# The ending of a cross-attention kernel: one power on GpSimd for root and reciprocal, block products ahead, half the bias by TensorE, two store queues

## The chip, the cores and the metric

The kernel runs on one core of a Trainium2 chip. The metric is the device time of one execution in microseconds (us), the median of the runs. The core has five engines that run side by side and wait for each other through semaphores: TensorE (PE; its weight loads are shown as PEld), VectorE (DVE), ScalarE (ACT), GpSimd (POOL) and SyncE (SP). SP, ACT and POOL have queues from which DMA transfers are issued (SPq, ACTq, POOLq in the profile).

## The reference

A batch of 8 inputs `x` (112 rows, 320 channels) attends to a context of 375 rows with 512 channels, of which the last 4 are prompts. There are 20 heads of 16 channels. Cut to what matters:

```python
q = heads(x @ W_q);  k_t = heads(text @ W_k);  v_t = heads(text @ W_v)
probs_t  = softmax(q @ k_t^T * scale)                  # over the 371 text rows
text_out = probs_t @ v_t
k_ip = heads(ip @ W_k_ip);  v_ip = heads(ip @ W_v_ip)  # the 4 prompts
qsem = l2norm(probs_t @ text)                          # x / max(|x|, 1e-12)
sem  = qsem @ l2norm(ip)^T
probs_ip = softmax(q @ k_ip^T * scale + 0.5 * sem) * spatial_mask
out = (text_out + probs_ip @ v_ip) @ W_out + b_out + x
```

## The kernel before

All of it is float32. The work is cut into 40 steps, 8 batches with 5 rounds of 4 heads each. In a round TensorE makes the scores, VectorE their maxima, ScalarE the exponentials `p` with a copy of each row's maximum taken off; a DMA and VectorE's 32x32 transposes turn `p` into `xgT`, and TensorE multiplies it (L761) with `u`, which holds for the batch the products of the context's rows with each other beside the prompts' normalised rows, a column of ones and the head's values. So one product gives, for a head, what is needed for the norm of `qsem` (first 371 columns, summed against `p` by VectorE in `reduced`, L814, into `ss`) and 21 value columns: 4 prompt similarities, the sum of the exponentials `z`, and 16 values. ScalarE copies these 21 into `pvs` (`value_sums`, L788).

PE, SP, DVE, ACT and POOL carry out the instructions in the order in which the program writes them: after the prologue the schedule is written by hand. Two generators write a batch's last part in pieces: `finish(b)` for batches 0 to 6 and `ending(b, bd)` for batch 7, advanced by `run(before, ...)` and `next(last)` at the end of the program, where batch 6's remaining pieces and batch 7's are dealt out between each other.

What the ending does for batch 7, with the names that the prediction uses:

- `divided` (L951): the values over `z` into `attn`; first for 16 heads on GpSimd, then for the last 4 on VectorE.
- `turned_attention` (L966): TensorE transposes `attn` by chunks of 128 channels into `ps_a` (two full ones first, the third later), ScalarE copies them to `aT`.
- `bd` holds the prompts' values, each head's block in its own rows. TensorE transposes it (`ps_bT`, L984), ScalarE copies it (`bT`), and TensorE multiplies the blocks by `W_out` (`ps_bw`, L1004), copied to `bw`. With it the prompts' part of the output is a single product of the prompt weights and `bw`.
- The prompts' softmax: `z2` (GpSimd), `rn` = max(z2 * eps^2, ss) on VectorE (L993), its root on ScalarE (L994) with the table of functions switched back to Exp behind it (L995), its reciprocal on VectorE (L1018), then four operations on `fu`, Exp on ScalarE (`ex`, L1025), and three operations to the weights `w` (L1033). TensorE transposes `w` (L1037), ScalarE copies it (`wT`, L1039).
- `projected` (L1010): `aT` times `W_out` into two halves of 160 columns, `ps_o_0` and `ps_o_1`, over the full chunks first and the third later; then `wT` times `bw` on top (L1042).
- VectorE adds the input with the bias (`xb`, which lies in a part of the tile named `bd`) to each half (L1047), and SP stores each (L1048).

Between these stand batch 6's last pieces: GpSimd's sums into `attn` (L903), its transposes (L908), its copy (L912), its product with `W_out` (L917) and its output sum (L923).

PSUM tiles are handed out by the pools `mm`, `sc` and `qd` in turn; a new tile waits until the readers of the bank's last tile are done.

Of the kernel before, what the change touches and what calls it, by code (L numbers as in the profile page):

```python
# [8 lines left out]
F32 = mybir.dt.float32  # L9
AF = mybir.ActivationFunctionType  # L10
ALU = mybir.AluOpType
# [3 lines left out]
NIP = 4  # L15
SEM_SCALE = 0.5
EPS = 1e-12
# [3 lines left out]
def kernel(  # L21
# [14 lines left out]
    nc = tc.nc  # L36
    P = 128
# [13 lines left out]
    RG = 32  # L51
# [177 lines left out]
    for i in range(NX):  # L229
        xt = const.tile([P, QN, TP], F32, tag=f"xg_{i}", name=f"xg_{i}")  # L230
        nc.gpsimd.memset(xt, 0.0)
        x_ring.append(xt)

    attn_ring = []
    for i in range(2):
        attn_ring.append(const.tile([S, CP], F32, tag=f"attn_{i}", name=f"attn_{i}"))
# [2 lines left out]
    def more_constants():  # L239
        halves(1)  # L240
        halves(2)
        nc.gpsimd.memset(wo_sb[REST:, FULL, :], 0.0)
        for at in attn_ring:
            nc.gpsimd.memset(at[:, C:], 0.0)
# [685 lines left out]
    def ending(b, bd):  # L930


        s = st[b]
        eng = nc.gpsimd
        h0 = FULL * HC

        def sm(name):
            return small.tile([S, H], F32, tag=name, name=f"{name}_{b}", bufs=1)

        def sm4(name):  # L940
            return small.tile([S, H, NIP], F32, tag=name, name=f"{name}_{b}", bufs=1)
# [9 lines left out]
        def divided(on, part):  # L951
            n = part.stop - part.start
            nc.vector.reciprocal(zr[:, part], z[:, part])
            on.tensor_tensor(
                attn[:, :C].rearrange("p (h d) -> p h d", d=D)[:, part],
                pvs[:, part, NIP + 1 :],
                zr[:, part].unsqueeze(2).to_broadcast([S, n, D]),
                ALU.mult,
            )

        divided(eng, slice(0, h0))
        yield

        aT = work.tile([P, NC, S], F32, tag="aT", name=f"aT_{b}")

        def turned_attention(chunks):  # L966
            ps = bank(f"ps_a_{b}_{chunks.start}")
            for i in chunks:
                nc.tensor.transpose(
                    ps[:, i * S : (i + 1) * S], attn[:, i * P : (i + 1) * P], ident[:S, :S]  # L970
                )
            at = slice(chunks.start, chunks.stop)
            nc.scalar.copy(
                aT[:, at],
                ps[:, at.start * S : at.stop * S].rearrange("p (i s) -> p i s", s=S),
            )

        turned_attention(range(FULL))
        yield


        ps = bank("ps_bT", spare=True)
        for i in range(NC):
            nc.tensor.transpose(  # L984
                ps[:, i * HN : (i + 1) * HN], bd[:HN, i * P : (i + 1) * P], ident[:HN, :HN]
            )
        bT = work.tile([P, NC, 2 * S], F32, tag="xT", name="bT", bufs=1)[:, :, :HN]
        nc.scalar.copy(bT, ps[:, : NC * HN].rearrange("p (i k) -> p i k", k=HN))
        yield

        z2, rn = sm("z2"), sm("rn")
        eng.tensor_tensor(z2, z, z, ALU.mult)
        nc.vector.scalar_tensor_tensor(rn, z2, EPS * EPS, s["ss"], ALU.mult, ALU.max)  # L993
        nc.scalar.activation(rn, rn, AF.Sqrt)  # L994
        nc.scalar.preload_act_table(AF.Exp)  # L995
        divided(nc.vector, slice(h0, H))
        yield

        turned_attention(range(FULL, NC))
        ps_bw = bank("ps_bw")  # L1000
        for i in range(NC):

            own = slice(i * RG, min((i + 1) * RG, HN))
            nc.tensor.matmul(  # L1004
                ps_bw[own, :C], bT[:, i, own], wo_sb[:, i, :], start=True, stop=True
            )
        ps_o = [bank(f"ps_o_{b}_0", spare=True)]
        ps_o.append(ps_qd.tile([P, 512], F32, tag="qd", name=f"ps_o_{b}_1"))

        def projected(chunks):  # L1010
            for ps, part in zip(ps_o, parts):
                for i in chunks:
                    nc.tensor.matmul(  # L1013
                        ps[:S, part], aT[:, i, :], wo_sb[:, i, part], start=(i == 0), stop=False
                    )

        projected(range(FULL))
        nc.vector.reciprocal(rn, rn)  # L1018
        fu, ex, w = sm4("fu"), sm4("ex"), sm4("w")
        nc.vector.tensor_tensor(fu, pvs[:, :, :NIP], over_ip(rn), ALU.mult)  # L1020
# [4 lines left out]
        nc.scalar.activation(ex, fu, AF.Exp)  # L1025
        bw = work.tile([S, NIP, H, D], F32, tag="wv", name="bw", bufs=1)
        bw = bw.rearrange("p n h d -> p n (h d)")[:HN, 0, :]
        nc.scalar.copy(bw, ps_bw[:HN, :C])
        yield

        nc.vector.tensor_reduce(sx, ex, AX.X, ALU.add)
        nc.vector.reciprocal(rx, sx)
        nc.vector.scalar_tensor_tensor(w, ex, sm_sb, over_ip(rx), ALU.mult, ALU.mult)  # L1033
        yield

        ps = bank(f"ps_wT_{b}")
        nc.tensor.transpose(ps[:HN, :S], w.rearrange("s h n -> s (h n)"), ident[:S, :S])  # L1037
        wT = work.tile([P, NE, TP], F32, tag="ctxT", name=f"wT_{b}")[:, 0, :S]
        nc.scalar.copy(wT[:HN], ps[:HN, :S])  # L1039
        projected(range(FULL, NC))  # L1040
        for ps, part in zip(ps_o, parts):
            nc.tensor.matmul(ps[:S, part], wT[:HN], bw[:, part], start=False, stop=True)  # L1042
        yield

        ob = work.tile([S, C], F32, tag="xb", name=f"ob_{b}", bufs=1)
        for ps, part in zip(ps_o, parts):
            nc.vector.tensor_tensor(ob[:, part], ps[:S, part], s["xb"][:, part], ALU.add)  # L1047
            nc.sync.dma_start(out[b, :, part], ob[:, part])  # L1048
        del st[b]
        yield  # L1050

# [350 lines left out]
    for g in range(NG):  # L1402
        if g == 1:
            run(("f", b - 2), None)
        for j, _ in enumerate(multiplied(b, g)):
            coming(g, places.get(g, {}).get(j, ()))
            if g == 0 and j == 2:
                transposed(b, g + 1)
            if g == 1 and j == 2:
                run(before, None)  # L1410
                own_channels(bd)
                transposed(b, g + 1)
            if g == 1 and j == 4:
# [49 lines left out]
    run(before, None, 2)  # L1463
    drain(last)
# [44 lines left out]
```

## Time and profile before

| | us |
|---|---|
| median of 3 runs | 409.94 |
| lowest and highest run | 409.65, 410.64 |
| the profiled execution: its span, first to last instruction | 409.5 |
| busy: TensorE | 402.0 |
| busy: VectorE | 333.5 |
| busy: ScalarE | 191.4 |
| busy: GpSimd | 127.6 |

The profile names a group or an instruction by its line in the kernel, its engine, its operation and its tiles (out<-in). In a timeline the first number is the start in us from the span's beginning, the second the length; equal neighbours are merged, with the first start, the whole length and their number. A note in brackets gives the engine's idle time before it and who ended it. A float32 matrix product is two instructions on TensorE, a transpose is one. The chain of waits is followed back from the last instruction: at each step to what released it, or to the instruction before it on its engine.

Some groups of the same page that frame the ending, by line, engine and operation, with count, busy time and mean length of one:

```profile
L761 PE MATMUL ps_qd<-u,xgT 32*112 32x136 f32 (+11 forms) x3840 | 216.4, 352 | 1.5 <-POOL u L679 1.1
L814 DVE CUSTOM_DVE_ANT_0 p<-ps_qd,p 112x371 f32<-112x371 f32 x152 | 73.6, 541 | 12.1 <-ACT pvs L788 7.4
L788 ACT COPY pvs<-ps_qd 112x21 f32<-112x21 f32 x152 | 21.8, 200 | 56.7 <-DVE ss L814 50.4
```

### The profile page before, as it was taken

To read this page: it belongs to the slowest core of one execution; us is meant where nothing else is said; L and a number is where in the kernel's file an instruction comes from. 1 tells how busy PE (TensorE), PEld (TensorE's weight loads), DVE (VectorE), ACT (ScalarE), POOL (GpSimd) and SP (SyncE) were. 2 spreads that over 40 slices of the span, in tenths; PEclk is the share of its full clock that TensorE was granted. 3 is DMA by queue.
4 is the path that set the end of the run, shared out by engine and by line. 5 is a ranking of instruction groups with operands and counts; after the bars stand their busy time and mean duration, and the time that the engine had idled before them with its cause. 6 is when DMAs were issued, how large, how long until landed. Compare 5 with 4: busy or idle time off the path is not lost.

```text
span 409.5 us, 14124 instructions
## 1 busy us (share of the span) xinstructions
PE 402.0 (98%) x5603; PEld 316.1 (77%) x5603; DVE 333.5 (81%) x705; ACT 191.4 (47%) x676; POOL 127.6 (31%) x294
## 2 busy tenths in 40 slices
PE   8998999999999999999999999999999999999996
PEld 8866687978777877878686877778777878787894
DVE  4354589877999898896899898887799988878985
ACT  3253234344533743434643574333734485346763
POOL 7203311322281153011154136002037135104681
PEclk9999999999999999999999999999999999999999
DMA  8876957799666866677646776666756444666310
GB/s 234 166 188 170 231 145 193 170 196 208 150 162 163 215 141 177 156 165 163 180 115 167 177 174 161 166 160 161 180 152 173 114 123 121 191 159 179 106 49 28
DMA packets 59332, 65.83 MB, mean 161 GB/s; under 512 B 20165, under 2 KB 52793, under 8 KB 59268
## 3 DMA queue, kind: packets, MB, share of 16 engines
q1 hardware_dynamic: 55326, 59.11, 58.4%
q0 software_dynamic: 1456, 3.14, 3.5%
q10 hardware_dynamic: 2486, 2.69, 2.1%
q8 instruction: 44, 0.72, 0.8%
q14 instruction: 20, 0.16, 0.1%
HBM read 20.22 MB, written 5.22 MB: 62 GB/s over the span
## 4 chain that ended last, share of the span: by engine, by line
PE 92%; DMA 3%; SPq 2%; POOL 1%; ACT 1%; issue 0%; DVE 0%; POOLq 0%
PE ps_qd L761 44%; PE ps_v L598 12%; PE ps_k L559 10%; PE ps_g L529 7%; PE ps_s L713 6%; PE ps_q L391 3%; PE ps_o L917 3%; DMA wip<-in_L_xattn_W_v_ip_dram 3%; PE ps_k L576 2%; PE ps_g L491 1%; SPq L737 1%; PE ps_w L477 1%; PE ps_c L460 1%; SPq L543 1%; PE ps_q L373 1%; PE ps_o L1013 0%
## 5 line engine op out<-in xcount | busy, mean ns | idle before, releaser
L761 PE MATMUL ps_qd<-u,xgT 32*112 32x136 f32 (+11 forms) x3840 | 216.4, 352 | 1.5 <-POOL u L679 1.1
L761 PEld LDWEIGHTS ps_qd<-u,xgT 32*112 32x112 f32 x3840 | 178.1, 172 | 36.4 <-issue 7.1
L749 DVE STREAM_TRANSPOSE xgT<-xg 128x768 f32<-128x768 f32 (+1 forms) x63 | 123.1, 1972 | 5.4 <-DMA xg<-p 5.1
L730 ACT ACTIVATE p<-ps_s,nmx 112x371 f32<-112x371 f32 x160 | 85.7, 585 | 56.9 <-DVE nmx L726 55.7
L726 DVE TENSOR_REDUCE nmx<-ps_s 112x1 f32<-112x371 f32 x160 | 77.2, 534 | 30.8 <-PE ps_s L713 28.9
L679 POOL COPY u<-vr 128x64 f32<-128x64 f32 x120 | 26.8, 237 | 190.9 <-PE ps_qd L761 113.8
L814 DVE CUSTOM_DVE_ANT_0 p<-ps_qd,p 112x371 f32<-112x371 f32 x152 | 73.6, 541 | 12.1 <-ACT pvs L788 7.4
L713 PE MATMUL ps_s<-kT,qm 32*112 32x375 f32 (+1 forms) x320 | 62.6, 485 | 0.0
L598 PE MATMUL ps_v<-wv_sb,ctxT 128*128 128x320 f32 x192 | 55.6, 437 | 0.0
L788 ACT COPY pvs<-ps_qd 112x21 f32<-112x21 f32 x152 | 21.8, 200 | 56.7 <-DVE ss L814 50.4
L598 PEld LDWEIGHTS ps_v<-wv_sb,ctxT 128*128 128x128 f32 x192 | 35.7, 190 | 14.3
L559 PE MATMUL ps_k<-ctxT,wk_sb 128*128 128x371 f32 x128 | 43.5, 483 | 0.0
L559 PEld LDWEIGHTS ps_k<-ctxT,wk_sb 128*128 128x128 f32 x128 | 23.1, 190 | 13.4 <-issue 1.3
L713 PEld LDWEIGHTS ps_s<-kT,qm 32*112 32x112 f32 x320 | 28.1, 171 | 5.7 <-ACT ug L508 0.4
L529 PE MATMUL ps_g<-ctxT 128*32 128x119 f32 (+11 forms) x672 | 32.4, 338 | 0.0
L529 PEld LDWEIGHTS ps_g<-ctxT 128*32 128x32 f32 x672 | 27.6, 109 | 5.9 <-issue 2.5
L448 DVE STREAM_TRANSPOSE ctxT<-ct 128x512 f32<-128x512 f32 x21 | 22.4, 1082 | 6.0 <-DMA u<-ug 6.0
L605 ACT COPY vext<-ps_v 128x320 f32<-128x320 f32 x24 | 10.2, 426 | 33.1 <-PE ps_v L598 24.5
L732 ACT COPY ipl<-ps_s 112x4 f32<-112x4 f32 x140 | 24.3, 173 | 0.0
L513 POOL TENSOR_TENSOR ug<-ug,half 128x128 f32<-128x128 f32 (+1 forms) x24 | 10.6, 448 | 29.7 <-ACT ug L512 27.6
L566 ACT COPY kT<-ps_k 128x371 f32<-128x371 f32 x16 | 7.5, 469 | 23.2 <-PE ps_k L559 22.8
L896 POOL TENSOR_TENSOR wv<-vip,w 112x1280 f32<-112x1280 f32 (+1 forms) x8 | 17.5, 2184 | 0.3 <-DVE w L890 0.3
(152 smaller groups left out, 326.0 us busy)
## 6 DMA issues: line engine op xcount, KB each, us to landing
xg<-p SPq DMA_DIRECT2D x159, 162.3 KB
u<-ug SPq DMA_DIRECT2D x128, 99.0 KB
ct<-in_ctx_dram SPq DMA_DIRECT2D x28, 176.0 KB
vip<-vipd SPq DMA_DIRECT2D x7, 560.0 KB
vr<-vd SPq DMA_DIRECT2D x20, 120.0 KB
out_dram<-ob SPq DMA_DIRECT2D x7, 140.0 KB
vd<-vext ACTq DMA_DIRECT2D x12, 80.0 KB
vr<-vd SPq DMA_DIRECT2D x12, 80.0 KB
```

The lines of the kernel that those rows point to most:

```text
L448: nc.vector.transpose(ctxT[:, :, c * P : (c + 1) * P].rearrange("p e (j i) -> p j e i", i=RG), ct[:, some, :].rearrange("p j (k e) -> p j ...
L529: nc.tensor.matmul(ps[p * RG : (p + 1) * RG, s0 : T - t0], ctxT[:, e, t0 + q * RG : t0 + (q + 1) * RG], ctxT[:, e, t0 + s0 : T], start=(e ...
L559: nc.tensor.matmul(ps[:, :TT], wk_sb[:, e, i * P : (i + 1) * P], s["ctxT"][:, e, :TT], start=(e == 0), stop=(e == NE - 1),)
L598: nc.tensor.matmul(ps[:, :C], ctxT[:, e, c * P : (c + 1) * P], wv_sb[:, e, :], start=(e == 0), stop=(e == NE - 1),)
L679: nc.gpsimd.tensor_copy(region(b, c)[:, :, UV - c * P :], s["vr"][:, c * QN : (c + 1) * QN, g, :])
L713: nc.tensor.matmul(ps[:S, :w], qm[a * RG : (a + 1) * RG, i, r, j * S : (j + 1) * S], s["kT"][a * RG : (a + 1) * RG, i, :w], start=True, st ...
L726: nc.vector.tensor_reduce(nmx, ps[:S, :TT], AX.X, ALU.max, negate=True)
L730: nc.scalar.activation(p, ps[:S, :TT], AF.Exp, bias=nmx)
L732: nc.scalar.copy(s["ipl"][:, groups[g][a], :], ps[:S, TT:T])
L749: nc.vector.transpose(xT[:, j : j + n].rearrange("p j (k q) -> p q j k", q=QN), xg[:, :, j * RG : (j + n) * RG].rearrange("p q (j k) -> p ...
L761: nc.tensor.matmul(banks[a][:S, j * RG : UW], xT[a * RG : (a + 1) * RG, j, :S], region(b, c)[a * RG : (a + 1) * RG, p, q * RG :], start=(j ...
L814: nc.vector.tensor_tensor_reduce(out=p, in0=ps[:S, :TT], in1=p, scale=1.0, scalar=0.0, op0=ALU.mult, op1=ALU.add, accum_out=s["ss"][:, h : ...
```

## The change

It touches `more_constants` in the prologue, `ending`, and the last lines of the program. Seven things differ:

1. The last round's remaining value columns (`value_sums(b, g, 0, 1)`) are copied ahead of the attention copies.
2. `bd`'s transposes stand ahead of batch 6's transposes, and the block products `ps_bw` behind these, ahead of batch 7's.
3. Root, function table and reciprocal are replaced by one `pow` of two tensors on GpSimd, with a constant tile `root` of -0.5. Both loads of ScalarE's function table in the ending (L995, and L1438 in round 3) go.
4. The last four heads' division moves from VectorE to GpSimd, behind the power, and their transposition behind the first products of the projection.
5. Half of the bias and input (`xb`, columns 160 to 319) is added by TensorE, as a product with the identity that opens `ps_o_1`.
6. That half is then copied by ScalarE and stored from ScalarE's queue; the other half stays with VectorE and SP.
7. Batch 6's output sum on VectorE stands behind batch 7's `w`.

```diff
+    root = const.tile([S, H], F32, tag="root", name="root")
...
     def more_constants():
         halves(1)
         halves(2)
+        nc.gpsimd.memset(root, -0.5)
...
-        divided(eng, slice(0, h0))
-        yield
-
+        divided(slice(0, h0))
+        ps = bank("ps_bT", spare=True)
+        for i in range(NC):
+            nc.tensor.transpose(
+                ps[:, i * HN : (i + 1) * HN], bd[:HN, i * P : (i + 1) * P], ident[:HN, :HN]
+            )
+        yield
+
+        bT = work.tile([P, NC, 2 * S], F32, tag="xT", name="bT", bufs=1)[:, :, :HN]
+        nc.scalar.copy(bT, ps[:, : NC * HN].rearrange("p (i k) -> p i k", k=HN))
+        yield
+
+        z2, rn = sm("z2"), sm("rn")
+        eng.tensor_tensor(z2, z, z, ALU.mult)
+        yield
+
+        ps_bw = bank("ps_bw")
+        for i in range(NC):
+
+            own = slice(i * RG, min((i + 1) * RG, HN))
+            nc.tensor.matmul(
+                ps_bw[own, :C], bT[:, i, own], wo_sb[:, i, :], start=True, stop=True
+            )
...
-        eng.tensor_tensor(z2, z, z, ALU.mult)
-        nc.vector.scalar_tensor_tensor(rn, z2, EPS * EPS, s["ss"], ALU.mult, ALU.max)
-        nc.scalar.activation(rn, rn, AF.Sqrt)
-        nc.scalar.preload_act_table(AF.Exp)
-        divided(nc.vector, slice(h0, H))
-        yield
-
-        turned_attention(range(FULL, NC))
...
+        bw = work.tile([S, NIP, H, D], F32, tag="wv", name="bw", bufs=1)
+        bw = bw.rearrange("p n h d -> p n (h d)")[:HN, 0, :]
+        nc.scalar.copy(bw, ps_bw[:HN, :C])
+        yield
+
...
+        nc.tensor.matmul(
+            ps_o[1][:S, : C // 2], ident[:S, :S], s["xb"][:, parts[1]], start=True, stop=False
+        )
         projected(range(FULL))
-        nc.vector.reciprocal(rn, rn)
+        nc.vector.scalar_tensor_tensor(rn, z2, EPS * EPS, s["ss"], ALU.mult, ALU.max)
+        eng.tensor_tensor(rn, rn, root, ALU.pow)
...
         nc.scalar.activation(ex, fu, AF.Exp)
...
+        divided(slice(h0, H))
+        turned_attention(range(FULL, NC))
...
         ob = work.tile([S, C], F32, tag="xb", name=f"ob_{b}", bufs=1)
-        for ps, part in zip(ps_o, parts):
-            nc.vector.tensor_tensor(ob[:, part], ps[:S, part], s["xb"][:, part], ALU.add)
-            nc.sync.dma_start(out[b, :, part], ob[:, part])
+        low, high = parts
+        nc.vector.tensor_tensor(ob[:, low], ps_o[0][:S, : C // 2], s["xb"][:, low], ALU.add)
+        nc.sync.dma_start(out[b, :, low], ob[:, low])
+        nc.scalar.copy(ob[:, high], ps_o[1][:S, : C // 2])
+        nc.scalar.dma_start(out[b, :, high], ob[:, high])
...
-        if g == 3:
-            nc.scalar.preload_act_table(AF.Sqrt)
...
     next(last)
     value_sums(b, g, 1)
-    run(before, None)
+    next(last)
     reduced(b, g, 0, 1)
-    next(last)
     value_sums(b, g, 0, 1)
-    reduced(b, g, 1)
     next(last)
     run(before, None)
     next(last)
+    reduced(b, g, 1)
+    run(before, None)
```

TensorE's order from the last round's end on, before the change (`ps_a`, `ps_o` with one number are batch 6's, `ps_a_0`, `ps_a_2`, `ps_o_0`, `ps_o_1` batch 7's):

```order
L908 MATMUL ps_a_5725<-ident,attn_144 128x112 x3
L969 MATMUL ps_a_0_5733<-ident,attn_145 128x112 x2
L984 MATMUL ps_bT<-ident,bd 128x80 x3
L917 MATMUL ps_o_5747<-wo_sb,aT_5729 112x320 x3
L969 MATMUL ps_a_2_5759<-ident,attn_145 128x112
L1004 MATMUL ps_bw<-wo_sb,bT 32x320 x2
L1004 MATMUL ps_bw<-wo_sb,bT 16x320
L1013 MATMUL ps_o_0_5766<-wo_sb,aT_5732 112x160 x2
L1013 MATMUL ps_o_1_5767<-wo_sb,aT_5732 112x160 x2
L1037 MATMUL ps_wT_5792<-ident,w_5775 80x112
L1013 MATMUL ps_o_0_5766<-wo_sb,aT_5732 112x160
```

The same stretch with the change:

```order
L967 MATMUL ps_bT<-ident,bd 128x80 x3
L911 MATMUL ps_a_5737<-ident,attn_145 128x112 x3
L984 MATMUL ps_bw<-wo_sb,bT 32x320 x2
L984 MATMUL ps_bw<-wo_sb,bT 16x320
L992 MATMUL ps_a_0_5748<-ident,attn_146 128x112 x2
L920 MATMUL ps_o_5757<-wo_sb,aT_5741 112x320 x3
L1021 MATMUL ps_o_1_5762<-bd,ident 112x160
L1013 MATMUL ps_o_0_5761<-wo_sb,aT_5747 112x160 x2
L1013 MATMUL ps_o_1_5762<-wo_sb,aT_5747 112x160 x2
L992 MATMUL ps_a_2_5783<-ident,attn_146 128x112
L1042 MATMUL ps_wT_5792<-ident,w_5772 80x112
L1013 MATMUL ps_o_0_5761<-wo_sb,aT_5747 112x160
```

`ps_bT` and `ps_bw` moved ahead, the product with the identity (L1021) is new, and the third transposition `ps_a_2` moved from ahead of the first products of the projection to right ahead of `ps_wT`. ScalarE's order at the same place, before:

```order
L912 COPY aT_5729<-ps_a_5725 128x336
L973 COPY aT_5732<-ps_a_0_5733 128x224
L788 COPY pvs_4334<-ps_qd_4_0_5666 112x21
L988 COPY bT<-ps_bT 128x3x80
L994 ACTIVATE rn_5752<-rn_5752 112x20
L995 ACT_TABLE_LOAD
L973 COPY aT_5732<-ps_a_2_5759 128x112
L1025 ACTIVATE ex_5774<-fu_5773 112x80
L1028 COPY bw<-ps_bw 80x320
L1039 COPY wT_5794<-ps_wT_5792 80x112
```

And with the change:

```order
L973 COPY bT<-ps_bT 128x3x80
L791 COPY pvs_4336<-ps_qd_4_0_5667 112x21
L915 COPY aT_5741<-ps_a_5737 128x336
L996 COPY aT_5747<-ps_a_0_5748 128x224
L1004 COPY bw<-ps_bw 80x320
L1033 ACTIVATE ex_5771<-fu_5770 112x80
L996 COPY aT_5747<-ps_a_2_5783 128x112
L1044 COPY wT_5794<-ps_wT_5792 80x112
L1054 COPY ob_5800<-ps_o_1_5762 112x160
L1055 DMA out_dram<-ob_5800 112x160
```

The copies of `bT`, of the last value columns and of `bw` moved ahead, the root and the table load are gone, the third attention copy stands behind Exp, and the second half's copy and store are new here.

More of the change, by code (lines that the diff above doesn't have):

```diff
@@ L949, in ending, with divided @@
         attn = attn_ring[b % 2]
-        def divided(on, part):
+        def divided(part):
             n = part.stop - part.start
             nc.vector.reciprocal(zr[:, part], z[:, part])
-            on.tensor_tensor(
+            eng.tensor_tensor(
                 attn[:, :C].rearrange("p (h d) -> p h d", d=D)[:, part],
@@ L978, in ending @@
         turned_attention(range(FULL))
+        bw = work.tile([S, NIP, H, D], F32, tag="wv", name="bw", bufs=1)
+        bw = bw.rearrange("p n h d -> p n (h d)")[:HN, 0, :]
+        nc.scalar.copy(bw, ps_bw[:HN, :C])
         yield
[L982 to L988, printed above, removed]
-        yield
[L991 to L995, printed above, removed]
-        divided(nc.vector, slice(h0, H))
-        yield
-        turned_attention(range(FULL, NC))
[L1000 to L1006, printed above, removed]
         ps_o = [bank(f"ps_o_{b}_0", spare=True)]
@@ L1013, in projected @@
                     nc.tensor.matmul(
-                        ps[:S, part], aT[:, i, :], wo_sb[:, i, part], start=(i == 0), stop=False
-                    )
+                        ps[:S, : C // 2],
+                        aT[:, i, :],
+                        wo_sb[:, i, part],
+                        start=(ps is ps_o[0] and i == 0),
+                        stop=False,
+                    )
+        nc.tensor.matmul(
+            ps_o[1][:S, : C // 2], ident[:S, :S], s["xb"][:, parts[1]], start=True, stop=False
+        )
         projected(range(FULL))
-        nc.vector.reciprocal(rn, rn)
+        nc.vector.scalar_tensor_tensor(rn, z2, EPS * EPS, s["ss"], ALU.mult, ALU.max)
+        eng.tensor_tensor(rn, rn, root, ALU.pow)
         fu, ex, w = sm4("fu"), sm4("ex"), sm4("w")
@@ L1025, in ending @@
         nc.scalar.activation(ex, fu, AF.Exp)
[L1026 to L1029, printed above, removed]
+        divided(slice(h0, H))
+        turned_attention(range(FULL, NC))
         nc.vector.tensor_reduce(sx, ex, AX.X, ALU.add)
@@ L1041, in ending @@
         for ps, part in zip(ps_o, parts):
-            nc.tensor.matmul(ps[:S, part], wT[:HN], bw[:, part], start=False, stop=True)
+            nc.tensor.matmul(ps[:S, : C // 2], wT[:HN], bw[:, part], start=False, stop=True)
         yield
         ob = work.tile([S, C], F32, tag="xb", name=f"ob_{b}", bufs=1)
-        for ps, part in zip(ps_o, parts):
-            nc.vector.tensor_tensor(ob[:, part], ps[:S, part], s["xb"][:, part], ALU.add)
-            nc.sync.dma_start(out[b, :, part], ob[:, part])
+        low, high = parts
[3 more added lines that the diff above has]
+        nc.scalar.dma_start(out[b, :, high], ob[:, high])
         del st[b]
```

## The prediction

> **What bounds the kernel now.** I read the page first, for the span.
>
> ```profile
> span 409.5 us, 14124 instructions
> ```
>
> The change leaves the main loop alone, so only the ending can move. Next I read the chain of waits in its last stretch (start, length, what; PE is TensorE).
>
> ```profile
> 399.62 0.60 POOL attn L954
> 400.22 0.04 issue
> 400.26 0.41 PE ps_a L969 x2
> 400.67 0.21 PE ps_bT L984 x3
> 400.88 1.70 PE ps_o L917 x6
> 402.58 0.10 PE ps_a L969
> 402.68 0.66 PE ps_bw L1004 x4
> 403.34 1.27 PE ps_o L1013 x8
> 404.61 0.09 issue
> 404.70 0.27 PE ps_wT L1037
> 404.96 0.55 PE ps_o L1013 x4
> 405.51 0.33 PE ps_o L1042 x2
> ```
>
> From 400.26 to 405.84 the chain is TensorE's own work, end to end, with 0.09 us of gap. Beside it runs a second chain, the prompt softmax, through GpSimd (POOL), VectorE (DVE) and ScalarE (ACT). First VectorE's part of it, from its timeline (start, length, engine, line).
>
> ```profile
> 401.06 0.08 DVE L814 DVE_READ_ACCUMULATOR2_ANT ss<- 112x1 f32 x1
> 401.47 0.18 DVE L993 SCALAR_TENSOR_TENSOR rn<-z,ss 112x20 f32<-112x20 f32 x1 [0.33 <-POOL z L992]
> ...
> 402.25 0.24 DVE L1020 TENSOR_TENSOR fu<-pvs,rn 112x80 f32<-112x80 f32 x1
> ...
> 404.25 0.30 DVE L1033 SCALAR_TENSOR_TENSOR w<-ex,sm_sb,rx 112x80 f32<-112x80 f32 x1
> ```
>
> The last row sum ends at 401.14, the weights w are ready at 404.55, and TensorE transposes them at 404.70, right after it ran out of other work at 404.61. Both chains arrive within 0.1 us of each other. So a shorter softmax alone gains nothing: TensorE must come free sooner too. The question is what the change does to each, and which is last afterwards.
>
> **The change part by part.**
>
> *Blocks of the prompts' values ahead.* The three bT transposes go in front of batch 6's own transposes, which wait for GpSimd.
>
> ```profile
> 395.62 3.48 PE L761 MATMUL ps_qd<-u,xgT 32*112 32x328 f32 x80
> 399.67 0.51 PE L908 MATMUL ps_a<-ident,attn 112*128 112x112 f32 x3 [0.57 <-POOL attn L903]
> ```
>
> The last product ends at 399.10 and L908 starts at 399.67, so 0.21 us of bT fits in that 0.57 us idle gap; without the gap it would cost its 0.21 again. ScalarE's timeline has the copies and the table load:
>
> ```profile
> 400.95 0.18 ACT L788 COPY pvs<-ps_qd 112x21 f32<-112x21 f32 x1
> 401.02 0.37 ACT L988 COPY bT<-ps_bT 128x240 f32<-128x240 f32 x1
> 401.68 0.22 ACT L994 ACTIVATE rn<-rn 112x20 f32<-112x20 f32 x1 [0.29 <-DVE rn L993]
> 401.92 1.28 ACT L995 ACT_TABLE_LOAD   x1
> 403.21 0.25 ACT L973 COPY aT<-ps_a 128x112 f32<-128x112 f32 x1
> 403.36 0.27 ACT L1025 ACTIVATE ex<-fu 112x80 f32<-112x80 f32 x1
> ...
> 405.00 0.25 ACT L1039 COPY wT<-ps_wT 80x112 f32<-80x112 f32 x1 [1.06 <-PE ps_wT L1037]
> ```
>
> The bT copy (0.37) now runs at about 399.55 to 399.93, in time for bw, which follows L908 at 400.18. So TensorE runs: bw 0.66, two attention transposes 0.20 (0.10 each when queued, as the third took in the chain), batch 6's projection 1.70. Before, the two transposes stood bare at 0.41 with a wait in front; now bw covers GpSimd's 0.60 us of L954, which ends at 400.22. That gives 400.18 + 0.66 + 0.20 + 1.70 = 402.74.
>
> *Half the bias by TensorE.* One more product of 160 columns, with the identity as weights. The chain shows 1.27 us for four such products and 0.55 for two, so about 0.30: 403.04. The first eight L1013 instructions: 404.31. The third attention transpose, now behind them: 404.41. Before, the same point was 404.61. TensorE gains 0.20 us.
>
> *The third transpose moved late.* It is not free where it now stands. Its result must be copied by ScalarE before the last two L1013 products can load their weights, and only the 0.27 us transpose of w lies between.
>
> ```profile
> 404.80 0.71 PE L1013 MATMUL ps_o<-wo_sb,aT 128*112 128x160 f32 x4
> 405.35 0.75 PE L1042 MATMUL ps_o<-bw,wT 80*112 80x160 f32 x4
> ```
>
> A lone transpose takes 0.27 (L1037), the copy starts 0.03 later (404.97 to 405.00) and takes 0.25, and the first product that uses such a copy starts 0.10 after its end (405.25 to 405.35). So 404.31 + 0.27 + 0.03 + 0.25 + 0.10 = 404.96, against 404.80 before. The 0.20 gained turns into 0.16 lost: what was hidden before (copy done at 403.46) is now a wait, and L1042 ends 0.16 later, at 406.26. The copy of wT, queued behind it on ScalarE, ends near 405.15 and is hidden by those two products.
>
> *Value columns copied sooner.* On ScalarE the last value copy moves ahead of two attention copies.
>
> It now starts at about 399.97, so GpSimd's square of z is done by 400.5 instead of 401.43. L993 then waits for the last row sum, which ends at 401.14, and starts at about 401.18 instead of 401.47: 0.29 sooner. More is not to be had, since four row sums on VectorE precede it.
>
> *Root and reciprocal as one power.* Sqrt, its table load and the reciprocal go; GpSimd's power P comes, with a hand-over on both sides. Before, L993's start to the first fu took 402.25 - 401.47 = 0.78. Now it takes 0.18 + 0.03 + P + 0.05, so fu starts at 401.44 + P. From fu's start to w's end took 404.55 - 402.25 = 2.30, so w is done at 403.74 + P. The table load that goes here buys nothing more: it ended at 403.20, and exp started at 403.36, once its input came. The other one stood ahead of round 4's value copies, which wait for products that end at 399.10 anyway. Behind the power on GpSimd only the last 64 attention columns wait, on VectorE the fu chain; both are inside these sums.
>
> P is the unknown: no row has a power. From below, it costs a plain multiplication of its shape, z's square in L992, 0.22. The marginal price of one elementary pass follows from that and the attention product on the same engine.
>
> ```profile
> 399.57 0.63 POOL L954 TENSOR_TENSOR attn<-pvs,zr 112x256 f32<-112x256 f32 x1
> 401.21 0.22 POOL L992 TENSOR_TENSOR z<-pvs 112x20 f32<-112x20 f32 x1 [1.00 <-ACT pvs L788]
> ```
>
> (0.63 - 0.22) / 236 elements = 1.73 ns, and a fixed part of 0.19. From above I take a hundred such passes for each of 20 elements, 0.19 + 3.46 = 3.65. A logarithm, a product and an exponential in software are some 25 passes rather than one or a hundred: 0.19 + 25 x 20 x 0.00173 = 1.05. I take that; it is an estimate.
>
> [...]
>
> *Which is last.* The last L1013 products start at the later of 404.96 and wT's start plus 0.10. wT starts 0.15 after w (404.55 to 404.70), so the second is 403.99 + P. Against 404.80 the delay is the larger of 0.16 and P - 0.81. The power stays covered up to P = 0.97; beyond it each microsecond counts in full.
>
> *Two store queues.* Before, VectorE added both halves and SyncE (SP) issued both stores.
>
> ```profile
> 406.21 0.32 SPq L1048 DMA_DIRECT2D out_dram<-ob  x1
> 406.63 0.38 SPq L1048 DMA_DIRECT2D out_dram<-ob  x1
> ```
>
> ```profile
> L623 ACTq DMA_DIRECT2D vd<-vext x24: 333/534/946, 63.9 to 355.3; - x24
> ```
>
> ```profile
> L314 ACT COPY kv<-ps_kv 64x160 f32<-64x160 f32 x1 | 0.3, 287 | 0.0
> ```
>
> L1042 ended at 406.10, and the second store was issued 0.53 later. Now ScalarE starts its copy 0.03 after the product, takes 0.29 (L314's shape in columns) and issues some 0.03 later: 0.35, so 0.18 sooner. Its issue takes 0.33 to 0.53 where SyncE took 0.38; with 0.43 the gain is 0.13 (0.03 to 0.23 for the two ends). The transfer itself and the wait for its end remain: no transfer ran with it that a second queue could overtake. Batch 6's output addition moves behind w on VectorE and is issued near 405.3 at P = 1.05, clear of the last stores.
>
> *The constant root.* One memset more in the prologue, ahead of others on GpSimd, at most the 0.22 of a multiplication of its shape. GpSimd has idle time behind it.
>
> ```profile
> 51.01 0.23 POOL L315 COPY kv<-kv 32x64 f32<-32x64 f32 x1 [6.82 <-ACT kv L313]
> ```
>
> That 6.82 us takes it in; without it, 0.22 at most.
>
> *Sum.* The larger of 0.16 and P - 0.81, less 0.13: with P = 1.05, 0.24 - 0.13 = +0.11 us on the profiled span, 409.5 to 409.6. The median of the runs, 409.94, lies 0.44 above that span; the same distance gives 410.05, so I predict **410.1 us**. The cheap power gives 0.16 - 0.13 = +0.03.
>
> **The rivals.**
>
> *A. The power is long* (slower; chance 0.30). Place: between L993 and fu, where nothing covers it beyond P = 0.97. The end is 409.94 + P - 0.94. To pass the 0.3% (1.23 us, about what a measurement of this kernel tells from no change) P must exceed 2.17, some 57 passes; the upper end of 3.65 gives 412.65, P = 3 gives 412.0. [...] Against it: GpSimd's rows show 1.73 ns an element once started, so P has to be ten times the 0.22 of a multiplication.
>
> *B. The power pays a load of its code on first use* (slower; chance 0.03). The only load of that sort in the trace is ScalarE's table load, 1.28; on top of 1.05 that makes P = 2.33, and 411.3. Against it: GpSimd's first of the mask products in the prologue is not slow.
>
> ```profile
> L513 POOL TENSOR_TENSOR ug<-ug,half x24: 427/453/467, 12.5 to 334.9; 128x128 f32<-128x128 f32 x16, 128x115 f32<-128x115 f32 x8
> ```
>
> [...]
>
> *C. The late transpose does not hurt* (within 0.3%, chance 0.12). If TensorE's last products start right behind wT, at 404.41 + 0.10 = 404.51, the gain is 0.29 + 0.13 = 0.42, and 409.5. It needs P below 0.52 and no wait for ScalarE; the built order has that copy between them, which speaks against it.
>
> *D. Something outside these terms gives over 0.3%* (faster, chance 0.05). The last store's data is over before 408.5, and the span runs on to 409.5; only that tail, on another queue, could give some 1.2 us: 408.7. (Stretch, its length, five engines' busy time, clock, DMA share, GB/s.)
>
> ```profile
> 408.50:409.00 0.50, 0.00 (x0) 0.00 (x0) 0.00 (x0) 0.00 (x0) 0.00 (x0) 1.00 0.00 0
> ```
>
> *The change does what it says but is hidden* is the forecast itself: its three savings (0.20 on TensorE, 0.29 on the row sums' successor, 0.13 on the store) are eaten by the late copy and the power.
>
> **How the numbers follow.** Forecast, P up to 2.17: 0.50. A 0.30, B 0.03, C 0.12, D 0.05. Within 0.3%: 0.50 + 0.12 = 0.62. Slower: 0.33. Faster: 0.05. The range runs from 409.4 (C, with the spread of the runs) to 412.3 (P = 3.3): beyond it lie B's worst, the longest powers and D, together near 0.18.
>
> **What would show it.** Right: batch 6's transposes still at 399.67; bw at 400.2; the late copy of aT ending near 404.9 and the last L1013 products just behind it or behind wT; exp free of a table load; the ScalarE store issued about 0.35 after L1042. The duration of the one GpSimd row rn<-rn,root is P, and w should end at 403.74 + P. Wrong: TensorE idle between 400.2 and 404.4, a power over 2.2 us, a change in the main loop, or a tail after the last store other than about 2.9 us from its issue.

## The result, and the profile after

The changed kernel takes 415.5 us (median of 4 executions, 415.12 to 415.87) beside 410.3 us of the kernel before on the same chip (4 executions, 409.65 to 412.41). The ratio of the two kernels' times on this chip is 1.0104, 95% interval 1.0081 to 1.0127: slower by some 4.3 us, outside the predicted range of 409.4 to 412.3. (The two medians alone lie 5.2 us apart; the ratio with its interval is what is used here.) A second measurement on another chip (e11 below) gave 1.0080 [1.0063, 1.0097], 3.3 us.

The first row of the changed kernel's page, and its chain of waits over the ending:

```profile
span 413.8 us, 14129 instructions
```

```profile
402.51 0.19 DVE rn L1025
402.71 0.07 issue
402.77 3.59 POOL rn L1026
406.36 0.02 issue
406.38 0.25 DVE fu L1028
...
408.37 0.32 DVE w L1038
408.69 0.14 issue
408.82 0.26 PE ps_wT L1042
409.08 0.68 PE ps_o L1013 x4
409.77 1.08 PE ps_o L1047 x4
```

Before, this stretch of the chain was TensorE's own work from 400.26 on. Now it is the prompt softmax from end to end, and its largest piece is the power on GpSimd. TensorE is no longer in the chain until the weights `w` are there. Its timeline shows what it does meanwhile:

```profile
391.57 8.85 PE L764 MATMUL ps_qd<-u,xgT 32*112 32x360 f32 x182
400.35 0.43 PE L967 MATMUL ps_bT<-ident,bd 80*128 80x80 f32 x3
401.03 0.51 PE L911 MATMUL ps_a<-ident,attn 112*128 112x112 f32 x3 [0.25 <-POOL attn L906]
...
404.27 1.25 PE L1013 MATMUL ps_o<-wo_sb,aT 128*112 128x160 f32 x8
407.97 0.32 PE L992 MATMUL ps_a<-ident,attn 112*128 112x112 f32 x1 [2.44 <-POOL attn L957]
408.82 0.26 PE L1042 MATMUL ps_wT<-ident,w 112*80 112x112 f32 x1 [0.54 <-DVE w L1038]
408.92 0.85 PE L1013 MATMUL ps_o<-wo_sb,aT 128*112 128x160 f32 x4
409.56 1.27 PE L1047 MATMUL ps_o<-bw,wT 80*112 80x160 f32 x4
```

It is done with the first projection products at 405.52 and then waits 2.44 us for the last four heads' division, whose result the third transposition (L992) turns. That division stands behind the power on GpSimd, and its reciprocal on VectorE behind the first four `fu` operations:

```profile
407.37 0.17 DVE L956 RECIPROCAL zr<-pvs 112x4 f32<-112x4 f32 x1
407.62 0.29 POOL L957 TENSOR_TENSOR attn<-pvs,zr 112x64 f32<-112x64 f32 x1 [1.27 <-DVE zr L956]
408.32 0.25 ACT L996 COPY aT<-ps_a 128x112 f32<-128x112 f32 x1 [0.57 <-PE ps_a L992]
```

GpSimd is free at 406.35 and waits 1.27 us for that reciprocal. The copy of the transposed chunk ends at 408.57, 0.10 before `w` is ready.

The last two products (L1047, four instructions) take 1.27 us, where the same two took 0.75 before. The clock that was granted in those moments (stretch, its length, the engines' busy time, clock, DMA share, GB/s):

```profile
409.00:409.25 0.25, 0.25 (x4) 0.25 (x4) 0.07 (x1) 0.13 (x1) 0.00 (x0) 1.00 0.00 0
409.25:409.50 0.25, 0.25 (x3) 0.20 (x2) 0.00 (x0) 0.12 (x1) 0.00 (x0) 0.72 0.00 0
409.50:410.00 0.50, 0.50 (x4) 0.50 (x3) 0.00 (x0) 0.00 (x0) 0.00 (x0) 0.50 0.05 15
```

The clock falls to half at about 409.4, just ahead of the last products.

The two profiled executions, 409.5 and 413.8, add up so. The main loop's last product ends at 400.42 instead of 399.10: +1.3. From there to the end of `w` it is 8.25 (408.67 - 400.42) instead of 5.45 (404.55 - 399.10): +2.8. From `w` to the last product's end it is 2.16 (410.83 - 408.67) instead of 1.55 (406.10 - 404.55): +0.6, the clock. From there to the end of the span it is 2.97 instead of 3.40: -0.4, the stores. Together +4.3. I call what follows the main loop's last product "the ending": 10.4 before, 13.4 after, so 3.0 of the 4.3 lie in it, and 1.3 ahead of it.

### The profile page after: what moved, and what is told of

Read it like the earlier page. It is cut to its first block, busy times and chain, and to the rows that moved or that the text cites. A ratio compares the mean times of both kernels' runs of the same rounds, so it can differ in the third digit from the quotient of the medians.

```text
span 413.8 us, 14129 instructions
## 1 busy us (share of the span) xinstructions
PE 403.2 (97%) x5605; PEld 318.9 (77%) x5605; DVE 332.0 (80%) x702; ACT 189.5 (46%) x674; POOL 131.3 (32%) x297
## 4 chain that ended last, share of the span: by engine, by line
PE 88%; DMA 7%; DVE 1%; ACT 1%; POOL 1%; SPq 1%; issue 0%; ACTq 0%; POOLq 0%; DVEq 0%
PE ps_qd L764 44%; PE ps_v L601 12%; PE ps_k L562 9%; PE ps_s L716 6%; PE ps_g L532 6%; PE ps_q L394 3%; DMA wip<-in_L_xattn_W_v_ip_dram 2%; PE ps_o L920 2%; PE ps_k L579 2%; DMA xg<-p 2%; DMA vr<-vd 1%; PE ps_g L494 1%; POOL rn L1026 1%; DVE p L817 1%; DMA u<-ug 1%; DMA ct<-in_ctx_dram 1%
## 5 line engine op out<-in xcount | busy, mean ns | idle before, releaser
L562 PEld LDWEIGHTS ps_k<-ctxT,wk_sb 128*128 128x128 f32 x128 | 23.1, 190 | 13.4 <-issue 1.3
```

The source lines that it names most:

```text
L562: nc.tensor.matmul(ps[:, :TT], wk_sb[:, e, i * P : (i + 1) * P], s["ctxT"][:, e, :TT], start=(e == 0), stop=(e == NE - 1),)
```

## The experiments

Every kernel is compared with the kernel before on its own chip; the ending is read from its profiled execution.

**e1, e2: the power alone, and all but the power.** e1 is the kernel before with only the root tile and the power; e2 is the changed kernel with the root, the table loads and the reciprocal back.

```diff
e1, against the kernel before
+    root = const.tile([S, H], F32, tag="root", name="root")
+        nc.gpsimd.memset(root, -0.5)
-        nc.scalar.activation(rn, rn, AF.Sqrt)
-        nc.scalar.preload_act_table(AF.Exp)
+        eng.tensor_tensor(rn, rn, root, ALU.pow)
-        nc.vector.reciprocal(rn, rn)
-        if g == 3:
-            nc.scalar.preload_act_table(AF.Sqrt)
```

> The kernel before with the power alone: the root on ScalarE, both table loads and the reciprocal replaced by the power on GpSimd; everything else as before. Theory (the power itself is the loss): the power takes 3.6 us, w ends 3.58 + 0.08 - 0.60 = 3.1 us later than before counted from the last product's end, TensorE idles over 2 us ahead of the weights' transpose and its clock falls, 0.6 more: 3.1 to 3.7 us above the kernel before. Rival 1 (the loss lies in the rest of the change, and in the stretch ahead of the ending): under 2 us above before.

> The changed kernel without the power and its constant: root on ScalarE, table loads and reciprocal as before, all other parts of the change kept. Theory (the power is the loss): within 0.5 us of the kernel before, TensorE's clock at full to the end. Rival 1 (the other parts lose too): 1.3 us or more above before, seen as a later end of the last product or as TensorE idle between 400 and 404.

e1: 414.12 us, ratio 1.0088 [1.0049, 1.0128], ending 13.0. e2: 410.64 us, ratio 1.0006 [0.9987, 1.0026], ending 10.1. The power and TensorE's wait for `w` in e1:

```profile
400.83 3.57 POOL L997 TENSOR_TENSOR rn<-rn,root 112x20 f32<-112x20 f32 x1 [0.29 <-DVE rn L996]
...
406.87 0.26 PE L1038 MATMUL ps_wT<-ident,w 112*80 112x112 f32 x1 [3.15 <-DVE w L1034]
```

The power carries the loss by itself; the other parts together are worth 0.3 us in the ending, too little to show in the time. In e1 `w` is ready 2.9 us later than before, counted from the main loop's last product (8.33 instead of 5.45; 3.1 was expected). Its clock fell only at about 408.05, 0.3 before its last product was done, so of the 0.6 expected for the clock only 0.1 showed.

**e3: the root tile alone**, unused, in the kernel before. It costs one memset (0.12 us in the changed kernel), and by the author's reckoning, which no trace shows, moves every later tile by 96 bytes.

```diff
+    root = const.tile([S, H], F32, tag="root", name="root")
+        nc.gpsimd.memset(root, -0.5)
```

> The kernel before with the constant tile and its memset alone, not used: every tile allocated behind it lies 96 bytes further on, and GpSimd has one memset more. Theory (the later end of the last product, 400.40 against 399.10, is the difference of two executions): within 0.3 us of before, the last product ends at the same time as in other executions on this chip. Rival 2 (the shifted tiles slow transfers or reads all through the kernel): 1.0 to 1.5 us above before, and the last product ends about 1.3 later.

411.54 us, 1.0018 [0.9992, 1.0044]; ending 10.45, as before. Nothing in the ending, and no difference that can be told in the time.

**e4: the power in two halves**, ten heads each, to tell a price per element from a price of the first use.

```diff
-        eng.tensor_tensor(rn, rn, root, ALU.pow)
+        for some in (slice(0, 10), slice(10, H)):
+            eng.tensor_tensor(rn[:, some], rn[:, some], root[:, some], ALU.pow)
```

> The changed kernel with the power cut into two instructions of 10 heads each. Theory (a price per element, about 0.17 us each): two rows of 1.9 us each, together 3.7 to 3.8, the end 0.1 to 0.3 above the changed kernel. Rival 3 (a load of code or another price of the first use): the first row over 3 us, the second under 0.5.

415.04 us, 1.0113 [1.0063, 1.0163]. The tile `rn` in e4 and in the changed kernel (count, then the shortest, median and longest in ns):

```profile
L1027 POOL TENSOR_TENSOR rn<-rn,root x2: 1956/1976/1996, 401.7 to 403.6; 112x10 f32<-112x10 f32 x2
```

```profile
L1026 POOL TENSOR_TENSOR rn<-rn,root x1: 3576/3576/3576, 402.8 to 402.8; 112x20 f32<-112x20 f32 x1
```

Both halves take the same within 0.04 us (1.96 and 2.00), so no load of code at the first use shows. From these two sizes, (3.576 - 1.976) / 10 = 0.16 us for each element of a row, and 0.38 fixed, an estimate that takes the price as linear. With e4's 3.95 us in the two halves the ending is 13.06 and not longer than the changed kernel's 13.4: here TensorE's clock stayed at full speed until the last product was done (at 409.46; it fell at about 409.7).

**e5, e8, e7: where the tiles lie.** The tile of e3 with 64 floats instead of 20 (256 bytes, e5) or with 8 (32 bytes, e8), in the kernel before; and the changed kernel with its root tile padded to 64 floats (e7).

```diff
e5 and e8, against the kernel before
+    root = const.tile([S, 64], F32, tag="root", name="root")
+        nc.gpsimd.memset(root, -0.5)
...
+    root = const.tile([S, 8], F32, tag="root", name="root")
+        nc.gpsimd.memset(root, -0.5)
e7, against the changed kernel
-    root = const.tile([S, H], F32, tag="root", name="root")
+    root = const.tile([S, 64], F32, tag="root", name="root")[:, :H]
```

> The kernel before with an unused constant tile of 256 bytes and its memset: the tiles behind it keep their place within 64 and 256 bytes. Rival 2 in a sharper form (the 96 bytes of the constant put the large tiles off a 64-byte boundary, and their transfers are slower in the first 100 us): within 0.3 us of before. If the memset or the tile's mere presence cost the time: 0.7 us or more above before. If it is all the spread between executions: within 0.4 us either way, as with 32 bytes.

> The same with 32 bytes, which puts the tiles behind it off a 64-byte boundary as the change's 96 bytes do. Rival 2: 0.7 to 1.3 us above before, the ending itself (last product's end to the end of the span) unchanged at 10.4. Theory (spread between executions): within 0.4 us of before.

> The changed kernel with the constant tile padded to 256 bytes, so that only the ending differs from the kernel before. Theory (the power, 3.58 us, and what follows from it): the ending 13.0 to 13.4 us against 10.4, the whole 2.6 to 3.3 above before. If the 96 bytes cost nothing: as the changed kernel, 4 us above before.

On one chip: e5 411.09 us, 1.0004 [0.9987, 1.0020]; e8 412.14, 1.0021 [1.0004, 1.0039]; e7 414.58, 1.0082 [1.0060, 1.0105]. Their order is what a cost of misplaced tiles would give, but the intervals overlap. e7's ending is 13.9, longer than the 13.0 to 13.4 expected: its clock fell at about 407.5, before `w` was transposed. The main loop from 120 to 396 us of e5 and of e8, in one row each:

```profile
120.00:396.00 276.00, 275.79 (x4049) 215.89 (x4051) 241.61 (x505) 138.53 (x506) 87.07 (x180) 1.00 0.62 157
```

```profile
120.00:396.00 276.00, 275.11 (x4022) 216.00 (x4020) 240.24 (x503) 138.06 (x508) 86.76 (x182) 1.00 0.65 158
```

The DMA engines are busy 65% of this stretch with the shift by 32 bytes, 62% with the shift by 256, for about the same bytes (158 and 157 GB/s). Over all profiles of this case the same stretch gives 62 or 63% in the six whose tiles keep their places and 63 to 65% in the eight whose tiles are shifted: a lean, but the two groups touch. In e8 TensorE stands idle 0.7 us longer here; in the changed kernel and in e3, where the tiles are shifted too, it does not (275.81 busy, as in the kernel before). So no cost to TensorE that goes with the shift is shown in this stretch.

**e6: the root first.** e2's timeline on ScalarE shows why the softmax gained nothing there:

```profile
400.72 0.34 ACT L993 COPY aT<-ps_a 128x224 f32<-128x224 f32 x1 [0.56 <-PE ps_a L989]
400.77 0.18 DVE L1022 SCALAR_TENSOR_TENSOR rn<-z,ss 112x20 f32<-112x20 f32 x1
400.96 0.42 ACT L1001 COPY bw<-ps_bw 80x320 f32<-80x320 f32 x1
401.28 0.22 ACT L1023 ACTIVATE rn<-rn 112x20 f32<-112x20 f32 x1
```

`rn` is ready at 400.95, and the root starts at 401.28, behind two copies. The copy of `bw` is not needed before the last products. e6 is e2 with it behind Exp:

```diff
-        nc.scalar.copy(bw, ps_bw[:HN, :C])
         yield
...
         nc.scalar.activation(ex, fu, AF.Exp)
+        nc.scalar.copy(bw, ps_bw[:HN, :C])
```

> The changed kernel without the power, with the root on ScalarE ahead of the copy of bw (in the run without the power it stood behind it and started 0.33 after its input). Theory (without the power, w is last, and TensorE waits 0.5 us for it): root 0.2 us sooner, w 0.2 sooner, the ending 9.8 to 9.9 us against 10.4 before and 10.1 without the power; 0.3 to 0.6 us below before in the runs. Rival (TensorE's late third transpose is last): the ending stays at 10.1.

410.2 us beside 411.06, ratio 0.9981 [0.9966, 0.9996], ending 9.93. It is the only version measured faster than the kernel before, by 0.8 us, of which the ending explains 0.5; its interval lies below 1 by little, and it is one of many comparisons.

**e9, e10: TensorE kept busy during the power.** The changed kernel with three products more, whose results nobody reads, between the projection's first products and the third transpose. e9 writes them to a PSUM bank that waits for batch 6's output sum, e10 to one that is free.

```diff
e9
+        ps = bank("ps_fill", spare=True)
e10
+        ps = ps_qd.tile([P, 512], F32, tag="qd", name="ps_fill")
both
+        for _ in range(3):
+            nc.tensor.matmul(ps[:S, :C], ident[:S, :S], s["xb"][:, :C], start=True, stop=True)
         nc.vector.scalar_tensor_tensor(rn, z2, EPS * EPS, s["ss"], ALU.mult, ALU.max)
```

> The changed kernel with three idle products added on TensorE (320 columns each, the identity as weights, result read by nobody) between the projection's first products and the third transpose, so that TensorE works during most of the power. They add work of about 1.7 us (L917's six instructions of that size took 1.70) in a gap of 2.44 and so should delay nothing. Theory (the clock falls because TensorE stands idle for the length of the power): the granted clock stays at 1.00 to the last product; four output products take 0.75 instead of 1.27 and from wT's start to the last product's end go 1.3 us instead of 1.9; the ending (last product of the main loop to the end of the span) goes from 13.4 to about 12.8, and the time to about 414.9 on a chip where the kernel before takes 410.3, ratio about 1.009. Rival (the clock falls at a time after the last burst of products that this gap does not set, or for another reason): the four products still take 1.27 and the ending stays at 13.0 to 13.9.

> As e9_kept_busy, but the three idle products write a PSUM tile of the main loop's pool, whose readers are done by 401.5. In e9 their tile waited for batch 6's output sum, they began only at 407.64, 3.59 after the last product, at a clock that had fallen to 0.50 at about 406.75, and took 3.54 us instead of 1.7; the clock did not come back in the 6 us of work that followed. Now they should begin right behind the projection's first products, near 405.5, and end near 407.2, ahead of the third transpose. Theory (the clock falls because TensorE stands idle for most of the power): clock 1.00 to the last product, four output products 0.75 instead of 1.27, wT's start to the last product's end 1.3 us instead of 1.9, ending 12.8 instead of 13.4, time 414.9 where the kernel before takes 410.3 (ratio 1.009). Rival (the clock falls for another reason): four products still 1.27, ending 13.0 to 13.9.

e9 missed its aim: 419.62 us, 1.0191 [1.0149, 1.0233]. TensorE in its timeline and four of its stretches:

```profile
402.80 1.25 PE L1013 MATMUL ps_o<-wo_sb,aT 128*112 128x160 f32 x8
407.64 3.54 PE L1027 MATMUL ps_fill<-bd,ident 112*112 112x320 f32 x6 [3.59 <-DVE ob L926]
```

```profile
406.50:406.75 0.25, 0.00 (x0) 0.00 (x0) 0.22 (x2) 0.00 (x0) 0.00 (x0) 0.98 0.00 0
406.75:407.00 0.25, 0.00 (x0) 0.00 (x0) 0.21 (x2) 0.00 (x0) 0.00 (x0) 0.50 0.00 0
...
410.00:411.00 1.00, 1.00 (x4) 0.47 (x3) 0.00 (x0) 0.00 (x0) 0.00 (x0) 0.50 0.00 0
...
413.00:413.50 0.50, 0.50 (x4) 0.50 (x3) 0.00 (x0) 0.00 (x0) 0.00 (x0) 0.50 0.00 0
```

The products waited for DVE's L926, which the change had put behind `w`, and then stood in front of the third transpose. So the edit made what it was to prevent: TensorE idle from 404.05, the clock at half 2.7 us later, and everything after at half speed.

In e10 they run where they should:

```profile
403.88 1.78 PE L1027 MATMUL ps_fill<-bd,ident 112*112 112x320 f32 x6
406.49 0.32 PE L992 MATMUL ps_a<-ident,attn 112*128 112x112 f32 x1 [0.83 <-POOL attn L957]
407.33 0.26 PE L1045 MATMUL ps_wT<-ident,w 112*80 112x112 f32 x1 [0.53 <-DVE w L1041]
407.44 0.71 PE L1013 MATMUL ps_o<-wo_sb,aT 128*112 128x160 f32 x4
407.98 0.75 PE L1050 MATMUL ps_o<-bw,wT 80*112 80x160 f32 x4
```

```profile
408.00:408.50 0.50, 0.50 (x6) 0.48 (x4) 0.00 (x1) 0.00 (x0) 0.00 (x0) 1.00 0.05 15
```

Clock 1.00, the last two products in 0.75, ending 12.76 (411.7 - 398.94) where 12.8 was expected; 413.5 us, ratio 1.0052 [1.0031, 1.0073], where 1.009 was expected. Useless products make the changed kernel's ending 0.6 us shorter in the two profiles. One profile alone would not decide against the rival, since e4's clock stayed up without such products. But the granted clock of every execution, a mean over its span, agrees: 0.996 to 0.999 in the ten of e10, with a mean of 0.997, against 0.989 to 0.997 in the nine of the changed kernel (e11 included), with a mean of 0.994. The ratio fell by more than these 0.6 us (0.15%) can give; the rest is not seen in the ending.

**e11, e12: the changed kernel and its padded form once more**, on one chip, without another edit.

> The changed kernel once more, beside e12 on the same chip. The ending is worth 3.0 us of the 4.3 by the two profiles (13.4 against 10.4 from the last product to the span's end), 0.73%; measured were 1.04% [0.81, 1.27]. Theory (the root tile of 80 bytes moves all later tiles off their 64-byte places, and that costs some 0.8 us): ratio again near 1.010, and at least 0.2% above e12. Rival (the rest lies in how the main loop's first 100 us happened to go in four executions): ratio 1.007 to 1.008, and within 0.1% of e12.

> The changed kernel with its root tile padded to 256 bytes, so that all later tiles keep their places modulo 64 bytes. Its ending was 13.9, 3.5 above the kernel before's, or 0.85%; measured were 0.82% [0.60, 1.05]. Theory (misplaced tiles cost 0.8 us): ratio near 1.008, at least 0.2% below e11. Rival (chance in the first 100 us): within 0.1% of e11.

e11: 414.38 us, 1.0080 [1.0063, 1.0097], ending 13.25. e12: 413.86 us, 1.0055 [1.0034, 1.0076], ending 14.0. The padded kernel is 0.25% below the other, as in the first pair (0.22%, there on two chips), though its ending is longer, because its clock fell earlier; but the level of e11 is the rival's. And e10, whose tiles are misplaced too, has 0.52%, no more than its ending explains (12.76 - 10.4 = 2.4 us, 0.57%). That misplaced tiles cost time is not settled: three pairs lean to some 0.2%, each within its intervals, and e10 speaks against it.

## Why the prediction was wrong

**The step that failed is the price of the power.** The prediction took 25 elementary passes, 1.05 us, between 0.22 and 3.65. The row has 3.58: the upper end. At 0.16 us an element that is 92 passes of the 1.73 ns that the multiplications on GpSimd showed. The 25 passes were the author's estimate for a logarithm, a product and an exponential in software; no run shows that count, nor that GpSimd works a power out in that way, and the price of a pass came from operations that do one thing to each element. The row lies within the bounds; the choice between them was wrong. That it lies so near the upper bound is luck: the hundred passes were a round number with no row behind it either. Whether the count or the length of a pass was wrong, one duration can't tell. Rival A, which got 0.30, is what happened. With P = 3.58 the prediction's own sum gives 412.6, just above its range. No run shows the worst of B that the range puts beyond it: with the one load in the trace, 1.28, B ends at 411.3, inside the range, and e4's halves show none.

**The formula around it held.** `w` was to end at 403.74 + P, which is 8.22 us after the main loop's last product with P = 3.58; it ended 8.25 after. The instruction that writes `rn` (L993 before, L1025 now) started 0.28 sooner after that product (2.09 against 2.37), where 0.29 was forecast. Hand-overs around the power took 0.08 and 0.03 (0.03 and 0.05 forecast), `fu` to `w` 2.29 (2.30), `wT` started 0.15 after `w`. So the path was right and one term of the sum mis-sized: delay P - 0.81 = 2.77 instead of 0.24.

**TensorE came free sooner than worked out, and the late transpose did not decide.** From L911's start to the last of the first eight L1013 products it took 4.49 us (401.03 to 405.52), where 4.64 was forecast; before, with the third transposition among them, it was 4.94. The third transposition was forecast right behind these products, at 404.41; it waited for the division of the last four heads, which the prediction called part of its sums and which stood in none. That cost nothing, since its copy ended 0.10 ahead of `w`. The delay of 0.16 for the late copy of `aT` was to set a floor where the power is short. e2, in which the softmax is as short as before, shows that it did not decide: that copy ended 0.23 ahead of `wT`'s start, and TensorE waited for `w`.

```profile
403.80 0.25 ACT L993 COPY aT<-ps_a 128x112 f32<-128x112 f32 x1 [0.58 <-PE ps_a L989]
403.83 0.30 DVE L1037 SCALAR_TENSOR_TENSOR w<-ex,sm_sb,rx 112x80 f32<-112x80 f32 x1
...
404.28 0.26 PE L1041 MATMUL ps_wT<-ident,w 112*80 112x112 f32 x1 [0.52 <-DVE w L1037]
```

So the softmax was the last to come in every version with the changed order but e9, and in e6 a softmax 0.2 us shorter (5.26 from the last product to `w`, 5.45 before) went with a faster kernel, the shorter stores included. In e6 the late copy begins to count: it ended 0.09 after `wT`'s start, and the next product started 0.14 behind that start instead of 0.10. The prediction's remark that a shorter softmax alone gains nothing was not tried by itself.

**The clock was not foreseen.** The prediction asked what an idle TensorE waits for, not what idling does to it. After 2.44 us without work the clock halved on the last products (1.00 to 0.50 at about 409.4), for 0.6 us; e10's trace (longest pause in the ending 0.83 us, clock 1.00) and the granted clock of its ten executions (mean 0.997, against 0.994 in the changed kernel's nine) show that the idleness was the cause. In six executions (the changed kernel, e1, e7, e9, e11, e12) the fall came 2.6 to 4.3 us after the long idle time began; in e4 it came 5.2 us after, when the last product was done, and cost nothing. The moment varies: 2.6 to 2.7 us in e7, e9 and e12, 3.8 in the changed kernel, 4.1 in e11, 4.3 in e1. What sets it, the traces do not show.

**The stores gained more.** 0.13 was forecast, with 0.23 as the upper end; from the last product to the end it was 2.97 instead of 3.40, so 0.43. ScalarE's issue came 0.36 after the product (0.35 forecast):

```profile
410.87 0.29 ACT L1054 COPY ob<-ps_o 112x160 f32<-112x160 f32 x1 [1.50 <-PE ps_o L1047]
411.19 0.34 ACTq L1055 DMA_DIRECT2D out_dram<-ob  x1
```

But from the issue to the end it took 2.6 us, where the second store on SP had taken 2.9; a tail other than 2.9 was one of the prediction's signs of being wrong. The second queue is not shown to be the reason. In e1 both stores are SP's, and the second

```profile
408.80 0.38 SPq L1049 DMA_DIRECT2D out_dram<-ob  x1
```

was issued 2.6 us before the end at 411.4 too, while e3, e5 and e8, also with both on SP, took 2.9. What shortens this tail stays open. P - 0.81 less this 0.43 and with the clock's 0.6 gives 2.9, against 3.0 measured in the ending.

**The sum joined two executions.** The prediction set the median 0.44 above the profiled span. In the profiled executions with their own time, the run lies some 1.7 us above its span (415.51 and 413.8; in e10 413.43 and 411.7). By that, the execution profiled before took some 411.2 us, not 409.94. Little hangs on it, since the forecast adds a difference to the median; but the time ahead of the ending differs much between executions. The main loop's last product ended between 398.2 us (e5) and 402.8 us (e3) in the fourteen profiles. The 1.3 us that the changed kernel's profile has ahead of the ending arise mostly in the first 100 us, where its TensorE was busy for 95.8 us and before for 96.8, 0.7 of that between 50 and 100 us. That stretch of the changed kernel, and of the kernel before:

```profile
50.00:100.00 50.00, 49.10 (x791) 43.02 (x781) 39.77 (x81) 19.08 (x71) 9.78 (x34) 1.00 0.85 181
```

```profile
50.00:100.00 50.00, 49.80 (x797) 42.55 (x791) 40.51 (x83) 20.12 (x78) 10.20 (x35) 1.00 0.82 183
```

Most of it is how one execution went: in e11, the changed kernel without any edit, the main loop's last product ended at 399.34, 1.1 sooner than in the first profile and 0.2 later than in the kernel before's. Its TensorE, too, was busy for only 96.0 us of the first 100. Whether the tiles' places add to it stays open.

## What to carry to other kernels

An operation that no row shows is priced by one measured row first, or else the forecast is carried by the upper bound; here the power cost 3.58 us for 20 elements a row, where root and reciprocal with their hand-overs had taken 0.60 (from 401.65 to 402.25). When an edit makes TensorE wait, ask also what the wait does to its clock: here the last products behind a gap of 2.44 us took 1.27 us instead of 0.75, and three idle products in the gap won that back (0.75 in e10), their PSUM bank being free; in e9, where it was not, they took 1.27. In an engine's order look first for what stands ahead of the critical instruction without being needed soon: the change without the power, and with one copy moved behind Exp, was the only version that gained.

## What the hardware showed beyond that

In e9 the clock did not come back before the end: TensorE worked from 407.64 to 414.18, 6.5 us with one pause of 0.15, at 0.50 throughout. In e3 it did come back: TensorE stood idle for 2.33 us up to 51.22, and the mean clock was 0.97 from 50 to 100 us and 1.00 from 100 to 120. In e7 and e12 the clock fell before `w` was transposed, in the changed kernel after that, in e4 only when all products were done: the same power costs 0 to 1.1 us more by where the fall comes.
